# Maxima by one-input reductions, statistics in other steps and second-norm factors in one place, in an attention and mixture-of-experts kernel

## The chip, the cores and the metric

The kernel runs on one core of a Trainium2 chip. The metric is the device time of one execution in microseconds (us); the time of a kernel is the median of several runs. Besides these runs there is one profiled execution, from which every view of the trace is taken; its own time stands beside its span below. The engines are called TensorE (PE, its weight loads PEld), VectorE (DVE), ScalarE (ACT), GpSimd (POOL) and SyncE (SP, which issues most transfers).

## The reference

```python
x = layernorm(x + attention(x))          # x: 4 x 1024 x 256, 16 heads of 16
x = layernorm(x + experts(x))            # 8 experts, top 2, capacity 640
# attention: softplus magnitudes times cos/sin of positions make q and k of 32 elements a head
scores = einsum('bhsd,bhtd->bhst', q_embed, k_embed) / D ** 0.5
out = einsum('bhst,bhtd->bhsd', softmax(scores), v)
# experts: a token goes to its two best experts, if these have a free slot
h = gelu(einsum('ecd,edh->ech', buf, w1) + b1)
out = einsum('ech,ehd->ecd', h, w2) + b2
```

Everything is float32. The layernorm has no learned scale. The second layernorm of a token that no expert took is again a norm of an already normed row, so that it needs only one factor for a row.

## The kernel before, in words

**Attention.** The work is cut into 32 units: 4 batches of 8, each with two heads and all 1024 queries in two halves. A unit has eight steps, one for each block of 128 keys; the loop over `NS` writes the order of every engine by hand. A step of unit u does, in this order: two halves of the scores of the *next* unit, with queries on the partitions (`score_half`, L701), a tile of this unit's scores with keys on the partitions (`key_scores`, L728), a third score half, the second tile, a fourth score half; then `exponentials` adds minus the maximum of each query to the tiles by a matmul with two rows (L743) and takes the exponential on ScalarE (L750); then `weighted_values` (L764, 16 matmuls) of the step before.

The scores of the next unit serve only to find each query's maximum: VectorE reduces each half from PSUM (L705, 512 keys to one number, negated) into the small tile `nm`. The score halves, and every other small matmul (embeddings, values, projections, transposes), share three PSUM banks that go round (`bank`), so that a score half waits until VectorE has reduced the one of three banks before.

In step 6 of a unit `max_parts` takes the smaller of the two halves' negated maxima (L711), rounds it to the float32r format of the matmul (L712), and takes the rest that the rounding left (L713); all three are on VectorE, 16 elements a partition. In step 7 `max_rows` transposes both parts (L719), and ScalarE copies them out of PSUM (L721) for the next unit's L743. `max_parts(0)` and `max_rows(0)` also stand ahead of the first step.

**Work beside it.** The table `todo` gives pieces of other work to fixed steps (unit p of the batch, step c). `embedding` makes the next batch's q and k in three stages: matmuls (L367) with ScalarE's softplus, then GpSimd's products and rounded parts (L390 to L405, operations of 128x512 on SBUF), then stores. `values` makes v (L336). `over_sums` divides by the softmax sums. `project` (L455) adds the output projection of two row tiles to the rows `x1` on VectorE (L463); `statistics` takes mean and variance of two row tiles (two of L472 and two of L473). For the second half of the heads of batch b-1 the four projections stand at (0,7), (1,0), (1,1), (1,2) of batch b, and the four `statistics` at (1,0), (1,1), (1,3), (1,4). Projections of the first half of the heads stand at (6,0) to (6,3), in the last batch at (5,2) to (5,5).

The list `FINISH` runs `finish_batch(b-1)` piece by piece after the `todo` of a step, from (1,5) on: the first norm's root (L495 to L502), the normed rows (L511), their transposes and the router's matmul, the softmax over experts, the two best experts, the slots by prefix sums (L600 to L606), and the scatters of rows into the experts' slots. At (3,7) it also starts `second_factors` (L665 to L669), which makes the factor of the second norm, `again`, for the rows that no expert takes; at (5,4) come the rest of it (L671 to L674) and the first scatter. Each of (5,4) to (6,3) converts the slot numbers of one row tile into integers on VectorE (L644) and issues two scatters from GpSimd (L646).

**End of attention.** For the last batch all this runs with no attention beside it: projections, statistics, and two interleaved `finish_batch` over four row tiles each (with `rotate`, which makes it use five banks, and convert the slot numbers at once); `second_factors` comes last in each.

**Experts.** For each of 8 experts the slots are loaded (L1071), transposed, multiplied by w1, gelu, w2. `without_experts` multiplies the normed rows by `again` (L1157) and stores them; rows of experts replace theirs later by scatters (L1191).

Of the kernel before, what the change touches and what calls it, by code (L numbers as in the profile page):

```python
# [10 lines left out]
F32 = mybir.dt.float32  # L11
F32R = mybir.dt.float32r
I32 = mybir.dt.int32
U32 = mybir.dt.uint32
AF = mybir.ActivationFunctionType
ALU = mybir.AluOpType
AX = mybir.AxisListType
# [3 lines left out]
P = 128  # L21
# [7 lines left out]
def kernel(  # L29
# [18 lines left out]
    nc = tc.nc  # L48
    B, S, DIM = x.shape
    E, _, HID = w1.shape  # L50
    HD = 16
    NT = S // P
# [49 lines left out]
    with ExitStack() as actx:  # L102
# [203 lines left out]
            return ps_3.tile([P, 512], F32, tag="bank", name=name)  # L306


        xts, qks, oss, ots, stats = {}, {}, {}, {}, {}
        nums, sums, routed, xt1s = {}, {}, {}, {}  # L310

        def transpose_x(b, i, rotate=False, copy=nc.scalar.copy):
# [152 lines left out]
            )  # L465

        def statistics(b, j):
            if b not in stats:
                stats[b] = small.tile([P, NT, 2], F32, tag="mv", name=f"mv_{b}")
            for t in (2 * j, 2 * j + 1):  # L470
                bs = small.tile([P, 6], F32, tag="bs", name=f"bs_{b}_{t}")
                nc.vector.bn_stats(bs, x1[:, b * NT + t, :])  # L472
                nc.vector.bn_aggr(stats[b][:, t, :], bs)  # L473

        def finish_batch(b, rotate=False, lo=0, n=NT):


            mv = stats[b][:, lo : lo + n, :]

            def some(name, shape):  # L480
                if (b, name) not in routed:
# [5 lines left out]
            def t1(name):  # L487
                return some(name, (NT,))[:, lo : lo + n]
# [2 lines left out]
                return some(name, (NT, E))[:, lo : lo + n, :]  # L491


            r, v, t = t1("ln_r"), t1("ln_v"), t1("ln_t")
            nc.vector.tensor_scalar(v, mv[:, :, 1], EPS, None, ALU.add)  # L495
            nc.scalar.activation(r, v, AF.Ln)
            nc.scalar.activation(r, r, AF.Exp, scale=-0.5)
# [131 lines left out]
            nc.vector.tensor_reduce(  # L629
                held[:, tiles, DIM : DIM + 2].rearrange("p t k -> p k t"), both, AX.X, ALU.add  # L630
            )
            second = second_factors(b, lo, n, r, v, t)
            if not rotate:
                next(second)
            yield
            if not rotate:
                next(second, None)
            for st in range(n):
                if st:
                    yield  # L640
                t = b * NT + lo + st
                if not rotate:

                    nc.vector.tensor_copy(scatter_idx[:, :, t], to[:, :, st])  # L644
                for k in range(2):
                    nc.gpsimd.indirect_dma_start(  # L646
                        out=scatter_views[2 * t + k],
                        out_offset=bass.IndirectOffsetOnAxis(
                            ap=scatter_idx[:, k, t : t + 1], axis=0
                        ),  # L650
                        in_=held[:, t, :],
                        in_offset=None,
                        bounds_check=SLOTS - 1,
                        oob_is_err=False,
                    )
            if rotate:
                yield
                for _ in second:
                    pass

        def second_factors(b, lo, n, r, v, t):


            more = again[:, b * NT + lo : b * NT + lo + n]
            nc.vector.tensor_tensor(v, r, r, ALU.mult)  # L665
            nc.vector.tensor_tensor(v, v, stats[b][:, lo : lo + n, 1], ALU.mult)
            nc.vector.tensor_scalar(v, v, EPS, None, ALU.add)
            nc.scalar.activation(more, v, AF.Ln)
            nc.scalar.activation(more, more, AF.Exp, scale=-0.5)  # L669
            yield  # L670
            nc.vector.tensor_tensor(t, more, more, ALU.mult)  # L671
            nc.vector.tensor_tensor(t, t, v, ALU.mult)
            nc.vector.tensor_scalar(t, t, -0.5, 1.5, ALU.mult, ALU.add)
            nc.vector.tensor_tensor(more, more, t, ALU.mult)  # L674

        zero = aconst.tile([P, ROW], F32, name="zero")
        nc.gpsimd.memset(zero, 0.0)
# [14 lines left out]
        def score_half(u, k, j):  # L692


            i, s = divmod(k, 4)
            if u not in nms:
                nms[u] = small.tile([P, 2, 4, 4], F32, tag="nm", name=f"nm_{u}")
            qk, h = qks[u], s % 2
            lo = HS * (s // 2) + P * i
            ps = bank(f"s_{u}_{k}_{j}")  # L700
            nc.tensor.matmul(  # L701
                ps, qk[:, 2 * h, lo : lo + P], qk[:, 2 * h + 1, j * HS : (j + 1) * HS],
                start=True, stop=True,
            )
            nc.vector.tensor_reduce(nms[u][:, j, i, s : s + 1], ps, AX.X, ALU.max, negate=True)  # L705

        def max_parts(u):

            nm = nms.pop(u)
            m = m_sb[u % 2].rearrange("p i (s c) -> p i s c", c=32)  # L710
            nc.vector.tensor_tensor(nm[:, 0], nm[:, 0], nm[:, 1], ALU.min)  # L711
            nc.vector.tensor_copy(m.bitcast(F32R)[:, :, :, 0], nm[:, 0])  # L712
            nc.vector.tensor_tensor(m[:, :, :, 1], nm[:, 0], m[:, :, :, 0], ALU.subtract)  # L713

        def max_rows(u, rotate=False):

# [135 lines left out]
        def run(pieces):  # L852
            next(pieces, None)
# [10 lines left out]
        for b in range(1, B):  # L864
            pieces = over_sums(b - 1, 1)
            for c in (1, 2, 5, 6):
                at(b, 0, c, run, pieces)
            for j, (p, c) in enumerate(((0, 7), (1, 0), (1, 1), (1, 2))):
                at(b, p, c, project, b - 1, 1, j)
            for j, (p, c) in enumerate(((1, 0), (1, 1), (1, 3), (1, 4))):  # L870
                at(b, p, c, statistics, b - 1, j)
        FINISH = [(1, 5), (1, 6), (1, 7), (2, 0), (2, 1), (2, 2), (2, 3), (2, 4), (2, 5), (2, 7)]
        FINISH += [(3, c) for c in range(NT)]
# [34 lines left out]
        with tc.manual_schedule():  # L908
            bias_angles()
            once("k", 0)  # L910
            for i in range(2):
                transpose_x(0, i, rotate=True)
            nc.scalar.dma_start(wv_sb, wv)
            for w in "kq":
                load_twice(w, 1, nc.scalar)
            key_table(0)
            once("q", 0)

            def first(w, h):
                tab = cs if w == "q" else kt0  # L920
                return embedding(0, 0, w, h, fast=True, tab=tab, pauses=(KC - 1,))

            k0, q0, k1, q1 = first("k", 0), first("q", 0), first("k", 1), first("q", 1)
            run(k0)
            for i in range(2, 4):
                transpose_x(0, i, rotate=True, copy=nc.vector.tensor_copy)
            for work in (q0, k0, q0, k0, k0):
                run(work)
            load_qk(0, halves[0], "k")
            for work in (k1, q0, q0):  # L930
                run(work)
            load_qk(0, halves[0], "q", nc.gpsimd)
            key_table(1)
            for work in (k1, q1, q1, k1, k1):
                run(work)
            load_qk(0, halves[1], "k")
            for work in (q1, q1):
                run(work)
            load_qk(0, halves[1], "q", nc.gpsimd)
            once("k", 1)  # L940
            once("q", 1)
            for h in range(2):
                values(0, 0, h, rotate=True)
            load_qk(1)
            for h in range(2):
                store_table(0, h, cs[:, :, halves[h]])
                store_table(1, h, kt0[:, :, halves[h]])
            late_constants()
            works = [embedding(0, 1, "q", h, tab=cs, pauses=(0, 1)) for h in range(2)]
            vals = [values_in_two(0, 1, h) for h in range(2)]  # L950
            beside = {n: (run, works[0]) for n in (3, 5, 6, 11, 17)}
            beside |= {n: (run, vals[i]) for n, i in ((8, 0), (10, 0), (14, 1), (16, 1))}
            beside |= {n: (second_key_table, h) for n, h in ((1, 0), (12, 1))}
            beside |= {n: (run, works[1]) for n in (20, 22, 23)}
            at(0, 0, 1, run, works[1])
            at(0, 0, 2, run, works[1])
            n = 0
            for queries in range(2):
                for keys in range(2):
                    for i in range(8):  # L960
                        score_half(0, 4 * (i // 2) + 2 * queries + i % 2, keys)
                        if n in beside:
                            f, *args = beside[n]
                            f(*args)
                        n += 1
            max_parts(0)
            max_rows(0, rotate=True)


        NS = B * NU * NT  # L970
        finishing = {}
        with tc.manual_schedule():
            for n in range(NS):
                u, c = divmod(n, NT)
# [13 lines left out]
                if ahead:  # L988
                    score_half(v, k, 0)
                    score_half(v, k, 1)  # L990
                tiles = [key_scores(u, c, 0)]
                if ahead and not third_last:
                    score_half(v, k + 1, 0)
# [10 lines left out]
                if n > 0:  # L1004
                    weighted_values(*divmod(n - 1, NT))
                if c == 6 and u + 1 < B * NU:
                    max_parts(u + 1)
                if c == 7 and u + 1 < B * NU:
                    max_rows(u + 1)
                if c == 1 and u > 0 and not by_rows(u - 1):  # L1010
# [10 lines left out]
        with tc.manual_schedule():  # L1021
# [27 lines left out]
                run(one)  # L1049
            for _ in two:  # L1050
                pass
            run(one)
            nc.scalar.preload_act_table_set("gelu_and_others")


# [292 lines left out]
```

## Time and profile before

| what | us |
|---|---|
| median of 3 runs (lowest to highest) | 1449.51 (1448.92 to 1450.37) |
| the profiled execution | 1455.47 |
| its span, first to last instruction | 1453.6 |
| of the span: start, up to the first step's L743 | 60.9 |
| the 256 steps, to the end of the last L764 | 60.9 to 1103.5 |
| from there to the first transpose of slots (L1082) | 1103.5 to 1153.9 |
| experts | 1153.9 to 1453.6 |
| granted TensorE clock, mean of the span | 0.972 |

A row of groups reads: line, engine, operation, output<-input, output shape<-input shape, count | busy us, mean ns of one | idle time of the engine just before, and what ended most of it. A row of the timeline reads: start in us, length in us, engine, line, operation, names and shapes, count, and in brackets the idle time before it with its releaser. Rows of neighbouring instructions of one kind are merged there. A busy TensorE is not TensorE at its peak, since the ends of matmuls are modelled. `min/median/max` of a line are the lengths of its single instructions.

The length of a step can be read from the timeline as the time from one first L743 to the next. The shortest with scores of a next unit is 3.50 us, in about 100 steps; at c = 7, which has `max_rows`, it is 3.87.

### The profile page before, as it was taken

How to read it: one execution, taken by the hardware profiler on the slowest of the kernel's cores; microseconds unless marked ns; L12 is line 12 of the kernel's file. 1: busy time of each engine (PE TensorE's matmuls, PEld its weight loads, DVE VectorE, ACT ScalarE, POOL GpSimd, SP SyncE). 2: the span in 40 equal slices, each digit the busy share in tenths (PEclk: the TensorE clock that was granted, in tenths of full speed). 3: DMA queues.
4: the chain of work that ended last, by engine and by line, in shares of the span. 5: the costliest groups of instructions: out<-in, count | busy, mean ns of one | idle time of the engine just before them, and what ended most of it. 6: DMA issues, size and time to landing. Idle time of an engine off the chain costs nothing. (4 is left out here: it accounts for less than half of the span.)

```text
span 1453.6 us, 24361 instructions
## 1 busy us (share of the span) xinstructions
PE 1367.7 (94%) x9314; PEld 859.4 (59%) x9314; DVE 921.3 (63%) x1990; ACT 727.5 (50%) x944; POOL 411.2 (28%) x436
## 2 busy tenths in 40 slices
PE   5899999999999999999999999999996399999996
PEld 3455555655665565555555555555543277777775
DVE  7767766667877766787767677887644433333334
ACT  5365666565566556546674654655553122222221
POOL 5640043340002637000064530000210414444542
PEclk8899999999999999999999999999998599999998
DMA  7956367373444646454465352224210436433211
GB/s 240 261 177 173 100 188 205 87 228 107 126 120 113 213 133 180 121 151 102 129 185 181 105 176 74 63 63 118 90 64 0 139 112 212 115 120 131 73 44 43
DMA packets 107315, 191.23 MB, mean 132 GB/s; under 512 B 19633, under 2 KB 56178, under 8 KB 107072
## 3 DMA queue, kind: packets, MB, share of 16 engines
q1 hardware_dynamic: 96192, 167.80, 39.7%
q0 software_dynamic: 9888, 20.01, 4.5%
q10 hardware_dynamic: 1120, 1.87, 0.4%
q8 instruction: 73, 1.20, 0.4%
q14 instruction: 42, 0.34, 0.1%
HBM read 119.32 MB, written 73.63 MB: 133 GB/s over the span
## 5 line engine op out<-in xcount | busy, mean ns | idle before, releaser
L705 DVE TENSOR_REDUCE nm<-s 128x1 f32<-128x512 f32 x1024 | 644.8, 684 | 230.4 <-PE s L701 212.6
L750 ACT ACTIVATE pt<-st 128x1024 f32<-128x1024 f32 x512 | 496.3, 1021 | 393.7 <-PE st L743 378.9
L701 PE MATMUL s<-qk 128*128 128x512 f32 x1024 | 391.5, 441 | 25.6 <-DVE nm L705 14.5
L728 PE MATMUL st<-qk 128*128 128x512 f32 x1024 | 308.4, 401 | 3.5 <-ACT pt L750 3.4
L764 PE MATMUL av<-pt,va 128*32 128x256 f32 x4096 | 275.5, 386 | 0.5 <-ACT pt L750 0.5
L701 PEld LDWEIGHTS s<-qk 128*128 128x128 f32 x1024 | 180.2, 191 | 138.3 <-DVE nm L705 62.4
L728 PEld LDWEIGHTS st<-qk 128*128 128x128 f32 x1024 | 183.3, 189 | 67.1 <-ACT pt L750 32.7
L764 PEld LDWEIGHTS av<-pt,va 128*32 128x32 f32 x4096 | 107.1, 109 | 107.8 <-issue 62.4
L646 POOL DMA_INDIRECT slots_in<-held,scatter_idx x64 | 62.7, 980 | 304.4 <-DVE scatter_idx L644 226.4
L390 POOL TENSOR_TENSOR soft_q<-y_q,soft_q 128x512 f32<-128x512 f32 x14 | 17.9, 1282 | 447.3 <-ACT soft_q L386 447.2
L1249 PE MATMUL op<-w,h 128*128 128x256 f32 x640 | 144.1, 379 | 0.0
L1230 PE MATMUL hp<-slots_t,w 128*128 128x320 f32 x512 | 139.9, 434 | 0.0
L743 PE MATMUL st<-mt,ones_r 2*128 2x512 f32 x1024 | 129.6, 495 | 0.7 <-ACT mt L721 0.7
L1249 PEld LDWEIGHTS op<-w,h 128*128 128x128 f32 x640 | 119.4, 190 | 15.9
L1230 PEld LDWEIGHTS hp<-slots_t,w 128*128 128x128 f32 x512 | 97.7, 191 | 40.0 <-ACT slots_t L1083 0.3
L743 PEld LDWEIGHTS st<-mt,ones_r 2*128 2x128 f32 x1024 | 49.0, 181 | 89.5 <-issue 88.1
L1237 ACT ACTIVATE h<-hp,b_sb 128x640 f32<-128x640 f32 x64 | 50.8, 794 | 86.6 <-PE hp L1230 73.3
L1264 DVE TENSOR_TENSOR o<-op,b_sb 128x256 f32<-128x256 f32 x35 | 14.9, 425 | 93.3 <-PE op L1249 88.9
L1265 ACT ACTIVATE o<-o,w 128x256 f32<-128x256 f32 x35 | 17.8, 507 | 103.1 <-issue 71.9
L1267 POOL DMA_INDIRECT y_rank<-o,rows x35 | 35.9, 1025 | 98.4 <-ACT slots_t L1083 42.2
L1191 POOL DMA_INDIRECT out_dram<-row,rows x40 | 41.0, 1025 | 44.6 <-DVE row L1146 14.3
L396 POOL TENSOR_TENSOR e_k<-soft_k,tab_k 128x512 f32<-128x512 f32 x28 | 35.4, 1286 | 46.3 <-DMA tab_k<-table 45.8
(210 smaller groups left out, 1030.6 us busy)
## 6 DMA issues: line engine op xcount, KB each, us to landing
qk<-embed_q SPq DMA_DIRECT2D x248, 128.0 KB
qk<-embed_k SPq DMA_DIRECT2D x124, 256.0 KB
embed_k<-parts_k SPq DMA_DIRECT2D x64, 256.0 KB
w<-in_w_dram SPq DMA_DIRECT2D x16, 1024.0 KB
embed_q<-parts_q SPq DMA_DIRECT2D x56, 256.0 KB
y_rank<-zero SPq DMA_DIRECT2D x8, 1024.0 KB
tab_k<-table SPq DMA_DIRECT2D x14, 512.0 KB
tab_q<-table SPq DMA_DIRECT2D x12, 512.0 KB
```

The lines of the kernel that those rows point to most:

```text
L646: nc.gpsimd.indirect_dma_start(out=scatter_views[2 * t + k], out_offset=bass.IndirectOffsetOnAxis(ap=scatter_idx[:, k, t : t + 1], axis=0) ...
L701: nc.tensor.matmul(ps, qk[:, 2 * h, lo : lo + P], qk[:, 2 * h + 1, j * HS : (j + 1) * HS], start=True, stop=True,)
L705: nc.vector.tensor_reduce(nms[u][:, j, i, s : s + 1], ps, AX.X, ALU.max, negate=True)
L728: nc.tensor.matmul(ps[:, f, :], qk[:, 2 * h + 1, c * P : (c + 1) * P], qk[:, 2 * h, f * HS : (f + 1) * HS], start=True, stop=False,)
L743: nc.tensor.matmul(tiles[h][:, f, :], ones_r[rows, :], mts[u][rows, :], start=False, stop=True,)
L750: nc.scalar.activation(pt, tiles[h], AF.Exp)
L764: nc.tensor.matmul(av[32 * s : 32 * (s + 1), cols], va[f][:, c, 2 * p + h, :], pt[h][:, s // 2, cols], start=(c == 0 and n == 0), stop=(c ...
L1191: nc.gpsimd.indirect_dma_start(out=out_views[t], out_offset=bass.IndirectOffsetOnAxis(ap=to[:, 0, t : t + 1], axis=0), in_=row[:, t, :], i ...
L1230: nc.tensor.matmul(ps[:, i, 0:half], w1_sb[:, k, c * P : (c + 1) * P], s_t[:, k, i * half : (i + 1) * half], start=(k == 0), stop=(k == KC ...
L1237: nc.scalar.activation(h_t[:, c, :].rearrange("p (i n) -> p i n", i=2), ps[:, :, 0:half], AF.Gelu, bias=b1_sb[:, e, c : c + 1],)
L1249: nc.tensor.matmul(ps, h_t[:, c, t * P : (t + 1) * P], w2_sb[:, c, :], start=(c == 0), stop=(c == HC - 1),)
L1267: nc.gpsimd.indirect_dma_start(out=y_views[e * ST + t], out_offset=bass.IndirectOffsetOnAxis(ap=to[:, 1, t : t + 1], axis=0), in_=o_sb, in ...
```

## The change

- `max_parts`: the two halves of `nm` now lie side by side, and one reduction of 128x32 to 128x16 takes the smaller. ScalarE makes the rounded part and a rounded negated copy beside the unrounded one, and in the next step, after the first two score halves, VectorE adds the pairs by a second reduction, which gives the rest.
- The conversion of slot numbers at (5,4) to (6,3) becomes a reduction over one element.
- `statistics` stand at (1,2), (1,3), (1,4), (1,5).
- The variances of all 32 row tiles and the roots of the first norm are kept in two tiles for all batches, and `second_factors` runs once for all 32 row tiles, at the end of attention.

```diff
+        stats = aconst.tile([P, B * NT, 2], F32, name="stats")
+        roots = aconst.tile([P, B * NT], F32, name="roots")
...
-            r, v, t = t1("ln_r"), t1("ln_v"), t1("ln_t")
+            r, v, t = roots[:, b * NT + lo : b * NT + lo + n], t1("ln_v"), t1("ln_t")
...
-            second = second_factors(b, lo, n, r, v, t)
-            if not rotate:
-                next(second)
-            yield
-            if not rotate:
-                next(second, None)
+            yield
...
-                    nc.vector.tensor_copy(scatter_idx[:, :, t], to[:, :, st])
+                    nc.vector.tensor_reduce(
+                        scatter_idx[:, :, t], to[:, :, st : st + 1], AX.X, ALU.max
+                    )
...
-            if rotate:
-                yield
-                for _ in second:
-                    pass
-
-        def second_factors(b, lo, n, r, v, t):
-
-
-            more = again[:, b * NT + lo : b * NT + lo + n]
-            nc.vector.tensor_tensor(v, r, r, ALU.mult)
-            nc.vector.tensor_tensor(v, v, stats[b][:, lo : lo + n, 1], ALU.mult)
+
+        def second_factors():
+
+            v, t = (small.tile([P, B * NT], F32, name=f"second_{i}", bufs=1) for i in range(2))
+            nc.vector.tensor_tensor(v, roots, roots, ALU.mult)
+            nc.vector.tensor_tensor(v, v, stats[:, :, 1], ALU.mult)
             nc.vector.tensor_scalar(v, v, EPS, None, ALU.add)
-            nc.scalar.activation(more, v, AF.Ln)
-            nc.scalar.activation(more, more, AF.Exp, scale=-0.5)
-            yield
-            nc.vector.tensor_tensor(t, more, more, ALU.mult)
+            nc.scalar.activation(again, v, AF.Ln)
+            nc.scalar.activation(again, again, AF.Exp, scale=-0.5)
+            nc.vector.tensor_tensor(t, again, again, ALU.mult)
             nc.vector.tensor_tensor(t, t, v, ALU.mult)
             nc.vector.tensor_scalar(t, t, -0.5, 1.5, ALU.mult, ALU.add)
-            nc.vector.tensor_tensor(more, more, t, ALU.mult)
+            nc.vector.tensor_tensor(again, again, t, ALU.mult)
...
-            nc.vector.tensor_tensor(nm[:, 0], nm[:, 0], nm[:, 1], ALU.min)
-            nc.vector.tensor_copy(m.bitcast(F32R)[:, :, :, 0], nm[:, 0])
-            nc.vector.tensor_tensor(m[:, :, :, 1], nm[:, 0], m[:, :, :, 0], ALU.subtract)
+            both = small.tile([P, 4, 4, 2], F32, tag="nm_parts", name=f"nm_parts_{u}")
+            nc.vector.tensor_reduce(both[:, :, :, 0], nm, AX.X, ALU.min)
+            nc.scalar.copy(m.bitcast(F32R)[:, :, :, 0], both[:, :, :, 0])
+            nc.scalar.activation(
+                both.bitcast(F32R)[:, :, :, 1], both[:, :, :, 0], AF.Copy, scale=-1.0
+            )
+            yield
+            nc.vector.tensor_reduce(m[:, :, :, 1], both, AX.X, ALU.add)
...
-            for j, (p, c) in enumerate(((1, 0), (1, 1), (1, 3), (1, 4))):
+            for j, (p, c) in enumerate(((1, 2), (1, 3), (1, 4), (1, 5))):
                 at(b, p, c, statistics, b - 1, j)
...
                     score_half(v, k, 0)
                     score_half(v, k, 1)
+                if parts:
+                    run(parts)
+                    parts = None
                 tiles = [key_scores(u, c, 0)]
...
                 if c == 6 and u + 1 < B * NU:
-                    max_parts(u + 1)
+                    parts = max_parts(u + 1)
+                    run(parts)
...
             for _ in two:
                 pass
-            run(one)
+            second_factors()
```

More of the change, by code (lines that the diff above doesn't have):

```diff
@@ L306, in bank @@
             return ps_3.tile([P, 512], F32, tag="bank", name=name)
-        xts, qks, oss, ots, stats = {}, {}, {}, {}, {}
+        xts, qks, oss, ots = {}, {}, {}, {}
+        stats = aconst.tile([P, B * NT, 2], F32, name="stats")
+        roots = aconst.tile([P, B * NT], F32, name="roots")
         nums, sums, routed, xt1s = {}, {}, {}, {}
@@ L467, in statistics @@
         def statistics(b, j):
[L468 to L473, printed above, removed]
+            for t in (b * NT + 2 * j, b * NT + 2 * j + 1):
+                bs = small.tile([P, 6], F32, tag="bs", name=f"bs_{t}")
+                nc.vector.bn_stats(bs, x1[:, t, :])
+                nc.vector.bn_aggr(stats[:, t, :], bs)
         def finish_batch(b, rotate=False, lo=0, n=NT):
-            mv = stats[b][:, lo : lo + n, :]
+            mv = stats[:, b * NT + lo : b * NT + lo + n, :]
             def some(name, shape):
@@ L696, in score_half @@
             if u not in nms:
-                nms[u] = small.tile([P, 2, 4, 4], F32, tag="nm", name=f"nm_{u}")
+                nms[u] = small.tile([P, 4, 4, 2], F32, tag="nm", name=f"nm_{u}")
             qk, h = qks[u], s % 2
@@ L704, in score_half @@
             )
-            nc.vector.tensor_reduce(nms[u][:, j, i, s : s + 1], ps, AX.X, ALU.max, negate=True)
+            nc.vector.tensor_reduce(nms[u][:, i, s, j : j + 1], ps, AX.X, ALU.max, negate=True)
         def max_parts(u):
@@ L965 @@
                         n += 1
-            max_parts(0)
+            for _ in max_parts(0):
+                pass
             max_rows(0, rotate=True)
         NS = B * NU * NT
-        finishing = {}
+        finishing, parts = {}, None
         with tc.manual_schedule():
```

## The prediction

> I write a step of the attention stage as (p, c): unit p of a batch, key block c; batch b is named where it matters. A step's length is the time between the first L743 matmuls of two neighbouring steps in the timeline.
>
> **What bounds the kernel now.** First the page's busy times and costliest groups:
>
> ```profile
> PE 1367.7 (94%) x9314; PEld 859.4 (59%) x9314; DVE 921.3 (63%) x1990; ACT 727.5 (50%) x944; POOL 411.2 (28%) x436
> ...
> L705 DVE TENSOR_REDUCE nm<-s 128x1 f32<-128x512 f32 x1024 | 644.8, 684 | 230.4 <-PE s L701 212.6
> L701 PE MATMUL s<-qk 128*128 128x512 f32 x1024 | 391.5, 441 | 25.6 <-DVE nm L705 14.5
> ```
>
> TensorE is the bound; among its waits, the one that this change can touch is L701's for L705: a score bank that VectorE has not yet reduced. The chain of waits covers only the last 25 us (output rows), so I went to the groups of all lines, looking at means that are far above what the same work takes elsewhere:
>
> ```profile
> L712 DVE CAST m<-nm 128x16 fp32r<-128x16 f32 x32 | 12.4, 388 | 1.1
> L713 DVE TENSOR_TENSOR m<-nm,m 128x16 f32<-128x16 f32 x32 | 10.8, 338 | 1.1
> L807 DVE RECIPROCAL den<-den 128x64 f32<-128x64 f32 x7 | 3.8, 544 | 0.8 <-DMA den<-sums 0.8
> L711 DVE TENSOR_TENSOR nm<-nm 128x16 f32<-128x16 f32 x32 | 9.6, 301 | 1.1
> L674 DVE TENSOR_TENSOR again<-again,ln_t 128x8 f32<-128x8 f32 (+1 forms) x5 | 2.9, 577 | 0.2
> L502 DVE TENSOR_TENSOR ln_r<-ln_r,ln_t 128x8 f32<-128x8 f32 (+1 forms) x5 | 0.8, 166 | 0.2
> ```
>
> L674 and L502 do the same arithmetic, yet one averages 577 ns and the other 166. By line, L711 takes 174/176/940 ns (min/median/max), L712 181/184/1233, L713 187/192/1202, L644 156/159/1299. The timeline shows where the long ones lie, here unit 7 of batch 2:
>
> ```profile
> 849.14 0.60 DVE L711 TENSOR_TENSOR nm<-nm 128x16 f32<-128x16 f32 x1
> ...
> 849.69 2.51 POOL L405 TENSOR_TENSOR parts_k<-e_k,parts_k 128x512 fp32r<-128x512 f32 x2
> 849.78 1.23 DVE L712 CAST m<-nm 128x16 fp32r<-128x16 f32 x1
> ...
> 851.05 1.20 DVE L713 TENSOR_TENSOR m<-nm,m 128x16 f32<-128x16 f32 x1
> 852.16 1.87 DVE L705 TENSOR_REDUCE nm<-s 128x1 f32<-128x512 f32 x3
> ...
> 852.90 0.49 PE L701 MATMUL s<-qk 128*128 128x512 f32 x1 [1.40 <-DVE nm L705]
> ```
>
> Each small VectorE operation lasts until a GpSimd operation beside it ends; the four reductions queue behind, and TensorE stands 1.40 us. The other kind of hole:
>
> ```profile
> 355.13 0.69 DVE L463 TENSOR_TENSOR held<-po,held 128x512 f32<-128x512 f32 x1 [1.41 <-PE po L455]
> ...
> 355.74 0.42 DVE L472 BATCH_NORM_STATS2 bs<-held 128x6 f32<-128x256 f32 x1
> ...
> 356.72 0.18 DVE L473 BATCH_NORM_AGGREGATE mv<-bs 128x2 f32<-128x6 f32 x1
> 356.82 1.85 DVE L705 TENSOR_REDUCE nm<-s 128x1 f32<-128x512 f32 x3
> ...
> 357.54 0.49 PE L701 MATMUL s<-qk 128*128 128x512 f32 x1 [0.82 <-DVE nm L705]
> ```
>
> No GpSimd is involved: the projection's addition comes late (it waits for TensorE), and the statistics behind it delay the next reductions.
>
> **What a step tolerates.** A plain step is 3.50 us; its four reductions take 2.48. Counted from L743, the fourth of the old step ends at +0.96, the first of the new one starts at +1.98: 1.02 us of VectorE are free. The fourth score needs the first one's bank: in the row above L701 starts 0.72 after the reductions (356.82 to 357.54), against +3.18 in a plain step, so they may be 0.48 late. Extra VectorE work up to 1.5 us costs nothing. That is why most long L711 to L713 are hidden: at (4,6) and (6,6), which carry an embedding's matmuls, steps of 5.20 are as long as at (4,2) and (6,4), without one.
>
> **The change part by part**
>
> *Statistics, from (1,0), (1,1), (1,3), (1,4) to (1,2) to (1,5).* Each issues four VectorE instructions (355.74 to 356.90, some 1.1 us) and no DMA. (1,0) and (1,1) of batches 1 to 3 last 5.43; a projection without statistics, at (6,1), takes 4.44. Six times 0.99 is 5.9 us. At (1,2), 6.13 long, the value matmuls (1.95 us) run behind the projection: the addition ends at 366.69, the next reduction starts at 368.02, and 1.1 fit between. At (1,3) and (1,4) such work stands today in steps of 3.50. (1,5) gets it beside L495 (0.2): 1.3 of the 1.5. ScalarE's L496 waits for L495, at about +2.3; its exponentials end at +2.55 anyway. Cost 0; without that cover 0.3 each. SP's queue has loads and zero fills at (1,4) and (1,5), which wait for none of this; GpSimd's has nothing there.
>
> *Second factors.* Today nine instructions per batch. Those at (3,7), two ScalarE ones among them, cost nothing (3.87, like any (p,7)). L671 to L674 and L644 at (5,4) do: 5.71 in batch 1 and 6.10 in batch 2, against 3.49 in batch 0, where they are absent; (5,5) follows with 3.87 and 5.07 against 3.50. Batch 3: 5.14 against 4.44 at its neighbour with the same projection. Gain (2.22 + 0.37) + (2.61 + 1.57) + 0.70 = 7.5 us. They come back once, 32 wide, after the last routing: 7 x 0.19 (row of 128x32) and 2 x 0.23 on ScalarE, some 2 us from 1137.7. The consumers, L1157, stand until the scatters have read their rows (1142.80 to 1149.39), and the expert stage waits for slots landing at 1153.9. GpSimd's last scatters wait for L629, which comes before; at (5,4) GpSimd's first scatter waits for L644, which now comes earlier. So 0; if not covered, +2.
>
> *Maxima.* Three VectorE operations per unit become one-input reductions, two of them, and two ScalarE operations. No tiny reduction of SBUF runs beside a GpSimd tensor operation here. Nearest row: L807, one input, SBUF to SBUF, 542/542/553 ns, though three of its seven lie beside L390 in the timeline. [...] Bounds: 0.17 to 0.2 us as L580 and L1096, or as long as L711's mean 0.30; I take 0.19. Gain at (7,6): 4.40, 5.05 and 5.16 become 3.50, that is 0.90 + 1.55 + 1.66 = 4.1. Batch 2's (7,7), 5.43, becomes 3.87: 1.6 more. At the start, max_parts(0) holds L719 from 57.33 to 59.13, 1.80 us; new chain 0.19 + 0.2 + 0.2 + 0.19 and three hand-overs of 0.05 is 0.93 (ScalarE idles there): 0.9.
>
> *The price of ScalarE.* Its small operations take 0.20 (L496) to 0.27 (L537). Both casts queue behind the exponentials, +2.55, and end at about +3.0. Behind them wait embedding reads of PSUM, which start 1.0 after ScalarE falls idle at (6,6), and the next exponentials at +4.1: 0. VectorE's second reduction comes in (p,7) after two score reductions, +3.2: 0.2 spare. Were it late, the third and fourth reductions are held; (p,7) is 3.87 long, and TensorE wants the third one's bank only 1.4 after its normal end.
>
> *scatter_idx.* Same count, 0.16 to 0.2 instead of a stall; counted at (5,4).
>
> [...] The long (7,7) of batch 2 and 1.2 us of (5,5) in batch 2 are not VectorE waits: the granted clock is 0.68 and 0.67 over these steps. [...] The gaps ahead of them are 1.40 and 2.35 us. [...] By the row, the falls directly follow two of the longest gaps, and the windows view has a clock of 1.00 in 100 to 700 and 900 to 1075 us, 0.98 only in between. I take the row.
>
> **Sum.** 5.9 + 7.5 + 4.1 + 1.6 + 0.9 = 20.0, less nothing: the span 1453.6 becomes 1433.6, and the profiled execution 1455.5 becomes 1435.5. The median of the runs shown, 1449.5, lies 6.0 below that execution; the steps are the same, so I take the difference over: 1429.5. What is late next in the freed steps is TensorE itself, at 3.50.
>
> **Rivals**
>
> 1. *Part of it stays* (0.16): the clock falls anyway, or the new reductions are stretched too. Then 2.8 is lost, or the 0.9 of the start and 1.1 of L644 at (5,4): about 1432.
> 2. *Another wait takes over at (5,4) and (7,6)* (0.06). For it: DMA is 0.64 to 0.74 busy in these holes. Against: L701 names L705, and its operands are loaded two units ahead. Only the statistics pay: 1443.6.
> 3. *ScalarE's casts come late* (0.03), slower. Place: VectorE, in order, stands at the second reduction of (p,7). It decides beyond 0.2 + 1.4 = 1.6 us of lateness; break-even at 20.0/31 = 0.65 more per unit. With the casts behind two further exponentials, 3 us late: 31 x 1.4 = 43, less 20: 1473. Against: the casts stand ahead of those exponentials in ScalarE's order.
> 4. *It cancels* (0.03): the same lateness of about 2.2 us: 1449.5.
>
> **How the numbers follow.** The forecast has 0.72. About 0.2% (3 us) is what a measurement of this kernel tells from no change. Faster is 0.72 + 0.16 + 0.06 = 0.94, same 0.03, slower 0.03. The range: down to 1425.5, since the clock's windows (3.4 us at half rate) can fall 1.7 us better on either side of the routing pause; up to 1437.5, past rival 1 with stalls of 3 us left and a second lost window.
>
> **What would show it.** (1,0), (1,1) at 4.44; (5,4), (5,5), (7,6) at 3.50 in batches 1 and 2; (1,3) to (1,6) still at 3.50; small reductions with a maximum near 0.2; no clock below 1 between 70 and 1090 us. Wrong if (p,7) exceeds 3.87, if VectorE waits for ScalarE there, or if the pause after attention grows.

## The result and the profile after

| what | us |
|---|---|
| kernel before, median of 5 runs beside it (lowest to highest) | 1450.37 (1448.92 to 1453.40) |
| kernel after, median of 5 runs | 1434.52 (1433.47 to 1435.21) |
| ratio, 95% interval | 0.9878 [0.9863, 0.9892] |
| profiled execution of after; its span | 1435.0; 1433.2 |
| predicted time (range); predicted span | 1429.5 (1425.5 to 1437.5); 1433.6 |

The kernel became 1.2% faster: 17.7 us by the ratio, while the two medians lie 15.9 apart. The predicted span was met to 0.4 us; the predicted median lies 5 us too low. The busy times and groups of the page after, the lines that answer to those of before (L697 was L705, L693 was L701):

```profile
PE 1360.3 (95%) x9314; PEld 856.8 (60%) x9314; DVE 888.3 (62%) x1930; ACT 732.8 (51%) x1000; POOL 410.5 (29%) x436
...
L697 DVE TENSOR_REDUCE nm<-s 128x1 f32<-128x512 f32 x1024 | 646.3, 684 | 240.5 <-PE s L693 232.2
...
L693 PE MATMUL s<-qk 128*128 128x512 f32 x1024 | 387.9, 438 | 13.6 <-DVE parts_q L408 8.3
```

What TensorE waits ahead of a score half falls from 25.6 to 13.6 us, and VectorE's reduction no longer leads that list (14.5 before; 2.1 by the groups of all lines). VectorE itself is 33 us less busy. The steps and the pause after them, by the windows view (borders, length; busy us and instructions of PE, PEld, DVE, ACT, POOL; granted clock; DMA share; GB/s), before:

```profile
60.90:1103.50 1042.60, 1024.49 (x7844) 596.61 (x7844) 735.71 (x1362) 608.80 (x732) 240.46 (x231) 0.99 0.47 135
1103.50:1153.90 50.40, 16.18 (x90) 11.39 (x90) 28.68 (x129) 7.88 (x20) 15.61 (x16) 0.64 0.15 49
```

and after:

```profile
60.10:1082.70 1022.60, 1017.45 (x7844) 594.37 (x7844) 704.33 (x1310) 614.09 (x788) 241.67 (x232) 1.00 0.48 138
1082.70:1133.10 50.40, 16.13 (x93) 11.08 (x91) 28.49 (x123) 7.56 (x18) 15.56 (x16) 0.61 0.15 49
```

The gain is in the 256 steps (20.0 us) and ahead of them (0.8); the experts take 299.7 us before and 300.1 after. The pause, where the second factors now stand, is as long as it was: they are hidden there. The small operations, by the single line's view (ns, min/median/max):

```profile
L704 DVE TENSOR_REDUCE nm_parts<-nm x32: 186/186/189, 58.0 to 1050.6; 128x16 f32<-128x32 f32 x32
```

```profile
L710 DVE TENSOR_REDUCE m<-nm_parts x32: 176/178/189, 58.6 to 1052.5; 128x16 f32<-128x32 f32 x32
...
  ACT nm_parts L706: 2.0, 2
```

No maximum above 0.19 us where L711 to L713 reached 0.94 to 1.23, although 17 of these 64 instructions ran beside a GpSimd tensor operation. VectorE waited for ScalarE's pair of casts only twice: 0.39 us at the start and 1.62 in the last unit, where it has no scores to reduce. The statistics' place, (1,0) of batch 1, which the prediction showed at 355 us, is now:

```profile
353.60 0.69 DVE L466 TENSOR_TENSOR held<-po,held 128x512 f32<-128x512 f32 x1 [1.43 <-PE po L458]
354.21 2.48 DVE L697 TENSOR_REDUCE nm<-s 128x1 f32<-128x512 f32 x4
```

The reductions follow the projection's addition at once, and the step fell from 5.43 to 4.38. Step (5,4) of batch 1, where the rest of the second factors stood, before:

```profile
502.25 1.18 DVE L674 TENSOR_TENSOR again<-again,ln_t 128x8 f32<-128x8 f32 x1
...
504.16 0.50 PE L701 MATMUL s<-qk 128*128 128x512 f32 x1 [1.95 <-DVE nm L705]
```

and after:

```profile
495.98 0.15 DVE L640 TENSOR_REDUCE scatter_idx<-to 128x2 uint32<-128x2 f32 x1
497.06 1.89 DVE L697 TENSOR_REDUCE nm<-s 128x1 f32<-128x512 f32 x3 [0.94 <-PE s L693]
```

TensorE waited for VectorE there; now VectorE waits for TensorE, and the step fell from 5.71 to 3.51. Unit 7 of batch 2, the place that the prediction showed at 849 us, now, VectorE, then GpSimd, then TensorE of the timeline:

```profile
835.40 0.19 DVE L704 TENSOR_REDUCE nm_parts<-nm 128x16 f32<-128x32 f32 x1
836.36 1.29 DVE L697 TENSOR_REDUCE nm<-s 128x1 f32<-128x512 f32 x2 [0.78 <-PE s L693]
```

```profile
835.11 1.16 POOL L406 CAST parts_k<-e_k 128x512 fp32r<-128x512 f32 x2
```

```profile
837.58 0.40 PE L693 MATMUL s<-qk 128*128 128x512 f32 x1
```

The reduction ends at 835.59, in the middle of GpSimd's casts (835.11 to 836.27), VectorE again waits for TensorE (0.78), and the fourth score starts with no wait in brackets. The step fell from 5.16 to 3.51. Not all is free of waits. One that was not there before, in (0,2) of batch 2:

```profile
853.46 0.55 DVE L804 RECIPROCAL den<-den 128x64 f32<-128x64 f32 x1 [1.97 <-DMA den<-sums]
...
854.61 0.49 PE L693 MATMUL s<-qk 128*128 128x512 f32 x1 [0.76 <-DVE nm L697]
```

VectorE waits 1.97 us at the division by the softmax sums until these are loaded, and its next three score reductions begin only behind it, at 853.93. The step took 0.55 more here and 1.0 more in batch 3.

### The profile page after: what moved, and what is told of

Read it like the earlier page. It is cut to its first block, busy times and chain, and to the rows that moved or that the text cites. A ratio compares the mean times of both kernels' runs of the same rounds, so it can differ in the third digit from the quotient of the medians.

```text
span 1433.2 us, 24396 instructions
## 1 busy us (share of the span) xinstructions
PE 1360.3 (95%) x9314; PEld 856.8 (60%) x9314; DVE 888.3 (62%) x1930; ACT 732.8 (51%) x1000; POOL 410.5 (29%) x436
## 5 line engine op out<-in xcount | busy, mean ns | idle before, releaser
L697 DVE TENSOR_REDUCE nm<-s 128x1 f32<-128x512 f32 x1024 | 646.3, 684 | 240.5 <-PE s L693 232.2
L693 PE MATMUL s<-qk 128*128 128x512 f32 x1024 | 387.9, 438 | 13.6 <-DVE parts_q L408 8.3
L693 PEld LDWEIGHTS s<-qk 128*128 128x128 f32 x1024 | 179.6, 190 | 121.4 <-DVE nm L697 49.9
L1251 PEld LDWEIGHTS op<-w,h 128*128 128x128 f32 x640 | 119.4, 190 | 15.9
```

The costliest lines, as they stand in the source:

```text
L693: nc.tensor.matmul(ps, qk[:, 2 * h, lo : lo + P], qk[:, 2 * h + 1, j * HS : (j + 1) * HS], start=True, stop=True,)
L697: nc.vector.tensor_reduce(nms[u][:, i, s, j : j + 1], ps, AX.X, ALU.max, negate=True)
L1251: nc.tensor.matmul(ps, h_t[:, c, t * P : (t + 1) * P], w2_sb[:, c, :], start=(c == 0), stop=(c == HC - 1),)
```

## The experiments

Theory 1 is the prediction's: each part takes away its own stalls, which are a constant of the kernel. Its rival, theory 2: the stalls change from one execution to the next, so that neither their sizes nor the 6.0 us between one execution and a median can be carried over. After the first four runs came theory 3: converting the slot numbers by a copy, beside GpSimd's scatters, holds the chip up, and only a kernel without it keeps its gains. The first four runs below were made on one chip, the next four on a second, the last four on a third; the kernel before had a median of 1455.47 us (37 runs, 1452.08 to 1461.82) on the first, 1453.06 (23 runs) on the second, 1454.35 (25 runs) on the third. A "hole" is a place where VectorE begins its reductions more than 0.3 us after the scores are done, with nothing in front of them.

**The kernel before, once more.**

> The kernel before, unchanged, profiled once more. The question: its first profiled execution took 1455.5 us, 5.1 over its median of 1450.4, so that a sum made against it promised 20 us where the runs gave 15.9. Theory 1: that one execution carried stalls that a usual one has not (half clock behind the two longest gaps in batch 2, 2.8 us; waits at (5,7) and (6,3) of batch 3, 1.9 us). Then this profiled execution takes 1449 to 1452, without some of those four, and all the other long steps, (1,0), (1,1), (5,4), (7,6), have the lengths they had within 0.1 us. Theory 2 (rival): the stalls beside GpSimd differ from one execution to the next as a whole; then (5,4) and (7,6) differ by 0.5 us and more. Ratio to before 1.000 within 0.001.

1454.29 us, ratio 0.9989 [0.9974, 1.0004]. The profiled execution took 1458.3, not the 1449 to 1452 that theory 1 expected. Its steps sum to 1041.7 (1042.6), but the stalls sit elsewhere: (5,4) of batch 2 takes 5.67 where it took 6.10, (7,6) of batch 2 4.04 for 5.16, (7,7) of batch 1 5.43 for 3.87, and the half clock falls at 509, 591 and 779 us in place of 773 and 855. Theory 2 holds for each stall; that their sum came out alike is one pair of executions. What made this one longer is the start: up to the first step's L743 it took 64.8 us, in place of 60.9.

**Statistics alone.**

```diff
-            for j, (p, c) in enumerate(((1, 0), (1, 1), (1, 3), (1, 4))):
+            for j, (p, c) in enumerate(((1, 2), (1, 3), (1, 4), (1, 5))):
```

> The kernel before with only the four statistics moved to (1,2) to (1,5). Both theories: (1,0) and (1,1) of batches 1 to 3 fall from 5.43 to 4.38, six times 1.05: 6.3 us less, in the runs too, since no GpSimd work is beside these steps. If the gain of the steps is given back later (a wait on a transfer), it is less than 5.

1450.3 us, ratio 0.9961 [0.9946, 0.9976], 5.7 us less. (1,0) and (1,1) of batches 1 to 3 take 4.37 to 4.38; (1,6) is 0.17 longer in each. This term of the sum (5.9) stands.

**Second factors alone.**

```diff
-            second = second_factors(b, lo, n, r, v, t)
...
+            second_factors()
```

> The kernel before with only the factors of the second norm made once for all tiles; the slot numbers are still converted by a copy. Theory 1: (5,4) of batches 1 and 2 fall to 3.5 to 4 us, 4 to 5 us less, and 0.7 in batch 3: 4.5 to 6 us in the runs. Theory 2: 2 to 4 us. The pause after attention is unchanged (50.5 us) by both; a rival in which the factors made there cost something gives 2 us more for it.

1455.13 us, ratio 0.9998 [0.9986, 1.0011]: no gain, a miss. And yet (5,4) of batches 1 and 2 is at 3.50 as expected. The profile shows where it went, in step (5,6) of batch 1:

```profile
510.20 0.71 PE L691 MATMUL s<-qk 128*128 128x512 f32 x2
...
511.36 0.97 POOL L642 DMA_INDIRECT slots_in<-held,scatter_idx  x1 [0.30 <-issue]
513.40 0.58 ACT L348 COPY va<-vp 128x512 f32<-128x512 f32 x1 [3.90 <-remote]
513.44 1.89 DVE L695 TENSOR_REDUCE nm<-s 128x1 f32<-128x512 f32 x3 [3.66 <-remote]
...
514.04 0.74 PE L691 MATMUL s<-qk 128*128 128x512 f32 x2 [2.20 <-ACT va L348]
```

The scores are done at 510.9; ScalarE and VectorE both start at 513.4, late and together, while GpSimd issues scatters, and the profile names no engine as releaser ("remote"). This step and (5,6) of batch 2 lost 2.5 us each; in batch 3 (5,7) and (6,0), at 5.60 and 5.06, lost 0.6 and 1.6 more. This led to theory 3.

**Maxima alone.**

```diff
-            nc.vector.tensor_tensor(nm[:, 0], nm[:, 0], nm[:, 1], ALU.min)
...
+            nc.vector.tensor_reduce(both[:, :, :, 0], nm, AX.X, ALU.min)
...
+            nc.vector.tensor_reduce(m[:, :, :, 1], both, AX.X, ALU.add)
```

> The kernel before with only max_parts changed to two one-input reductions and ScalarE's casts. Theory 1: (7,6) of batches 0 to 2 falls to 3.5, 4.1 us, and the start gains 0.3 to 0.8: 4 to 5 us in the runs. Theory 2: 2 to 3 us. If ScalarE's casts cost steps of their own, less than 2.

1451.46 us, ratio 0.9968 [0.9955, 0.9982], 4.7 us less. (7,6) takes 3.50, 3.79 and 3.50, (7,7) of batch 2 3.86; a new hole at (5,6) of batch 3 (4.55 in place of 3.49) and longer (5,5) in batches 1 and 2 (5.00 and 6.03, at half clock) take some of it back in the profiled execution.

**Conversion alone.**

```diff
-                    nc.vector.tensor_copy(scatter_idx[:, :, t], to[:, :, st])
+                    nc.vector.tensor_reduce(
+                        scatter_idx[:, :, t], to[:, :, st : st + 1], AX.X, ALU.max
+                    )
```

> The kernel before with only the conversion of the slot numbers changed, from a copy to a one-input reduction over one element. The factors alone gained nothing in the runs and the profile of that kernel has new holes of 2.5 us at (5,6), where TensorE's scores are done and VectorE and ScalarE start on them only 3 us later, while GpSimd issues scatters; such holes lie at (5,5) to (6,3) in every profile of a kernel with the copy and in none of the changed kernel. Theory 3 (new): the copy beside scatters in issue holds the chip up for 1 to 3 us at changing places; then this one edit takes 2 to 6 us off the runs and narrows their spread of 7 to 12 us to under 4, although its own time in the profile is worth 1.1. Theory 1: the edit is worth about 1 us.

1451.75 us, ratio 0.9991 [0.9979, 1.0003], 1.3 us, and its runs spread over 7.9 us: what theory 3 expected of it alone is missed. Its profile has no hole, and (5,4) falls to 4.73 and 5.03.

**The kernel after with the copy back.**

```diff
-                    nc.vector.tensor_reduce(
-                        scatter_idx[:, :, t], to[:, :, st : st + 1], AX.X, ALU.max
-                    )
+                    nc.vector.tensor_copy(scatter_idx[:, :, t], to[:, :, st])
```

> The changed kernel with the copy to integers put back in place of the reduction over one element, all else as changed. Theory 3: 3 to 8 us slower than the changed kernel on the same chip, with holes again at (5,5) to (6,3) and a spread of over 5 us. Theory 1: at most 1.2 us slower.

1434.89 us, ratio 0.9882 [0.9843, 0.9920]. The kernel after on this chip, two runs further down, has 0.9876: the intervals overlap. The copy takes up to 0.68 us, and no hole follows. On this chip the copy by itself does not hold the kernel up.

**The division one step later.**

```diff
-            for c in (1, 2, 5, 6):
+            for c in (1, 3, 5, 6):
```

> The changed kernel with the reciprocal of the softmax sums of the second heads at (0,3) in place of (0,2). Its profile shows VectorE waiting there for a load that now lands 1.5 to 2.0 us after VectorE reaches it, and steps of 4.05 and 4.51 in batches 2 and 3. If that is where part of the gain was given back, (0,2) is 3.50 again and the kernel is 1.0 to 1.6 us faster than the changed one. If the wait moves on to (0,3) or to the next load, 0 to 0.5.

1434.59 us, ratio 0.9879 [0.9843, 0.9916], no gain. (0,2) is at 3.49 in batches 2 and 3, but (0,5) of batch 1 takes 4.46 in place of 3.49: the wait moved to the load of the reciprocals, `r`, ahead of the multiplication (VectorE waits 1.72 us there).

**The kernel after, once more.**

> The changed kernel, unchanged, on the same chip as the three others, for comparison with them. Ratio to before 0.985 to 0.990; spread of its runs under 3 us; steps as in its first profile within 0.1 us, except that the waits for a load at (0,2) may differ.

1433.37 us, ratio 0.9876 [0.9840, 0.9913]; span 1430.9. Here (0,2) takes 4.02 in batch 1 and 3.48 in the others. So this wait, too, changes its place between executions, and e7 could not settle it.

**Factors and conversion together.**

```diff
-            second = second_factors(b, lo, n, r, v, t)
...
-                    nc.vector.tensor_copy(scatter_idx[:, :, t], to[:, :, st])
+                    nc.vector.tensor_reduce(
+                        scatter_idx[:, :, t], to[:, :, st : st + 1], AX.X, ALU.max
+                    )
...
+            second_factors()
```

> The kernel before with two parts of the change: second factors made once, and the slot numbers converted by a reduction; maxima and statistics as before. Theory 'the copy hides it' (the factors' gain was there in e3 but holes beside the scatters took it back, and these need the VectorE copy): (5,4), (5,5) of batches 1 and 2 at 3.50, no step between (5,5) and (6,3) over 4.0, and the runs about 6 us below the kernel before (6.0 from the steps of e3 plus some 0.3 to 1). Theory 'they are nearly nothing in runs': the sum of e3 and e5, 0.3 + 1.3 = 1.6 us below. Between 3 and 5 us would leave it open.

1445.62 us, ratio 0.9940 [0.9921, 0.9959]: 8.7 us less, where the two alone, on the first and the second chip, add up to 1.6. Its profile, at the place of the hole in the run of the factors alone:

```profile
509.29 0.97 POOL L644 DMA_INDIRECT slots_in<-held,scatter_idx  x1 [0.31 <-issue]
...
510.00 2.08 DVE L697 TENSOR_REDUCE nm<-s 128x1 f32<-128x512 f32 x3 [1.12 <-PE s L693]
```

The same steps and the same scatters, and VectorE is released by the score it waits for. (5,4) and (5,5) are at 3.50, and there is no hole. This is what a theory expects in which the copy brings the holes. But the run of the factors alone was made on another chip, so that the chip is a rival that this pair can't exclude.

**The second reduction as an operation of two inputs.**

```diff
-            nc.scalar.activation(
-                both.bitcast(F32R)[:, :, :, 1], both[:, :, :, 0], AF.Copy, scale=-1.0
-            )
...
-            nc.vector.tensor_reduce(m[:, :, :, 1], both, AX.X, ALU.add)
+            nc.vector.tensor_tensor(
+                m[:, :, :, 1], both[:, :, :, 0], m[:, :, :, 0], ALU.subtract
+            )
```

> The kernel after, with the second reduction of the maxima (step 7) replaced by a VectorE subtraction of two inputs, 128x16; ScalarE's negated copy is left out. Theory of the one-input form: this operation, and no other, is stretched beside GpSimd's 128x512 tensor operations, to a maximum of 0.9 to 1.3 us in the units with an embedding beside (7,7), while L704's reduction stays below 0.19. In time it costs nothing that the runs can tell (within 0.3% of the kernel after's ratio): the reductions behind it in a step (p,7) may be 1.4 us late. Rival, 'the form doesn't matter': its maximum stays below 0.25. Rival, 'no slack at (p,7)': the steps with a stretched subtraction exceed 3.87 by what it is longer, up to 1 us each, some 3 to 6 us in all.

```profile
L707 DVE TENSOR_TENSOR m<-nm_parts,m x32: 178/182/1237, 59.6 to 1051.7; 128x16 f32<-128x16 f32 x32
```

```profile
L704 DVE TENSOR_REDUCE nm_parts<-nm x32: 185/186/188, 59.2 to 1050.0; 128x16 f32<-128x32 f32 x32
```

The subtraction ran beside a GpSimd tensor operation in seven places and took 0.35 to 1.24 us in five of them (the longest at (4,7) of batch 0, not at (7,7) as expected). The reductions of the kernel after, beside the same GpSimd lines, take 0.189 us at most. It is not the number of inputs alone: L712 of the kernel before, a cast with one input, reached 1.23. The time is 1436.09 us, ratio 0.9873 [0.9843, 0.9903], as that of the kernel after; the step of the 1.24 takes 4.01, 0.14 more than 3.87. In a step of 3.87, behind two score reductions, even this is nearly covered.

**Extra VectorE work, two and three reductions of 128x512 in step 6.**

```diff
+                    for _ in range(2):
+                        idle = small.tile([P, 1], F32, tag="idle", name=f"idle_{u}_{_}")
+                        nc.vector.tensor_reduce(idle, wv_sb, AX.XY, ALU.max)
```

> The kernel after with extra work whose result nothing uses: two VectorE reductions of a 128x512 SBUF tile in step 6 of each unit, ahead of the maxima, about 0.62 each, 1.24 us. The prediction's tolerance: extra VectorE work up to 1.5 us in a step costs nothing; with the maxima's reduction (0.19) this is 1.43. Expected: (p,6) of the plain units at 3.50 to 3.55, the runs within 1.5 us of the kernel after. Rival, 'the tolerance is smaller' (1.0, the free time of VectorE alone): 0.4 in each of some 20 plain units, 8 us slower.

> The same with three such reductions, 1.86 us, with the maxima's 0.19 some 2.05: over the tolerance of 1.5 by 0.55. Expected: plain (p,6) at 4.0 to 4.1, TensorE waiting for L697's reduction there, and with some 20 such units the runs about 11 us above the kernel after (8 to 17, if the longer steps of the other units pay too). Rival, 'TensorE's place in the order hides more' (tolerance of 2.1 or more): within 1.5 us of the kernel after. Rival, tolerance 1.0: 1.05 a unit, 20 to 30 us.

The diff is that with two; with three the range is 3. Both add work that nothing uses. With two: 1441.94 us, ratio 0.9911 [0.9878, 0.9944]. The preceding run, as fast as the kernel after, was made on the same chip; against it this is 5.9 us more, where up to 1.5 was expected: missed. The plain units are as expected, (2,6) of batches 1 to 3 at 3.53 to 3.54, (7,6) at 3.48 to 3.51. Eleven others pay, 5.8 us in all, for instance (1,6) of batch 1 with 4.33. VectorE there:

```profile
378.29 1.27 DVE L1010 TENSOR_REDUCE idle<-wv_sb 128x1 f32<-128x512 f32 x2
...
379.57 0.16 DVE L500 TENSOR_TENSOR ln_t<-roots 128x8 f32<-128x8 f32 x1
...
380.25 1.28 DVE L697 TENSOR_REDUCE nm<-s 128x1 f32<-128x512 f32 x2
```

The first norm's root (L500 to L503, 0.7 us) stands in the same step. From 378.29 to 380.25 VectorE is held 1.96 us, over the tolerance of 1.5; the step is 0.84 longer, which leaves 1.1 for the tolerance here. The expectation counted the maxima and forgot what else stands in step 6: the root at (1,6), a multiplication by the reciprocal sums at (0,6) and, in batch 3, at (4,6), pieces of `finish_batch` at (3,6) and, in batch 3, at (5,6). With three, 1451.70 us, ratio 0.9985 [0.9975, 0.9995], 15.6 us more than that run (8 to 17 expected). (2,6) of batch 1, a plain one, takes 4.13, and TensorE shows the wait:

```profile
413.35 1.86 DVE L1010 TENSOR_REDUCE idle<-wv_sb 128x1 f32<-128x512 f32 x3
415.13 0.17 DVE L704 TENSOR_REDUCE nm_parts<-nm 128x16 f32<-128x32 f32 x1
```

```profile
415.96 0.50 PE L693 MATMUL s<-qk 128*128 128x512 f32 x1 [0.36 <-DVE nm L697]
```

The four operations hold VectorE from 413.35 to 415.30, 1.95 us, and plain steps are 0.40 to 0.63 longer, so the tolerance is 1.3 to 1.55 there: the prediction's 1.5 is near the upper end. Rivals at 1.0 and 2.1 both fall for plain steps.

## Why the prediction was right, and where it was not

| step of the prediction | predicted | profile after | that part alone, in runs |
|---|---|---|---|
| statistics | 5.9 | 6.3 | 5.7 [3.5, 7.9] |
| second factors and conversion | 7.5 | 7.5 | 8.7 [6.0, 11.5] |
| maxima at (7,6) and (7,7) | 5.7 | 5.6 | 4.7 [2.6, 6.5], with the start |
| start | 0.9 | 0.75 | |
| everything else | 0 | 0.3 | |
| sum | 20.0 | 20.4 | 19.1, together 17.7 [15.7, 19.9] |

Microseconds saved; the last column is one minus the ratio, times the median of before on that chip. The sum of 20.0 answers to two single executions, which differ by 20.4; against the 17.7 of the runs it lies just above the interval.

That the start came out as forecast is luck. Its operations of `max_parts(0)`, up to the first transpose, fell from 1.85 us (57.33 to 59.18) to 0.82 (57.99 to 58.81), but they began 0.66 later, and the start of one and the same kernel before took 60.9 and 64.8 in two executions.

**Which stalls go.** (5,4) and (5,5) of batches 1 and 2 are at 3.49 to 3.51 and (7,6) at 3.50 to 3.51; (5,4) of batch 3 is at 4.44, (7,7) of batch 2 at 3.87, (1,0) and (1,1) at 4.38. (1,3) to (1,6) stayed at 3.50. Each part alone shows its own, and the parts add up if factors and conversion are taken as one.

**The form of the operation.** The value taken for the reductions was 0.19, the measured ones 0.186 and 0.178; ScalarE's casts took 0.22 and 0.23, within the 0.20 to 0.27 assumed. The run with two inputs shows that a subtraction is stretched, up to 1.24 us, where a reduction in its place takes 0.189 at most. Why the one form is stretched and the other is not, no run shows.

**The clock.** The prediction put the two falls of the clock down to the gaps of 1.40 and 2.35 us ahead of them, and counted the 2.8 us that they cost as gained: 1.6 at (7,7) and 1.2 at (5,5) of batch 2. The windows view of before, over the two stretches at half clock:

```profile
772.50:776.20 3.70, 3.70 (x25) 2.21 (x22) 2.27 (x5) 1.94 (x2) 2.93 (x3) 0.54 0.16 55
854.50:858.10 3.60, 3.60 (x18) 2.79 (x11) 1.43 (x3) 1.96 (x3) 0.00 (x0) 0.53 0.78 215
```

and of after, over all steps but the first:

```profile
70.00:1082.00 1012.00, 1006.89 (x7818) 588.94 (x7817) 696.99 (x1299) 612.15 (x786) 239.56 (x230) 1.00 0.48 136
```

With these two gaps gone, the falls are gone. Had the clock fallen all the same, the 2.8 us would have been lost. The other traces agree: all ten falls between 75 us and the end of the steps, in six profiles, come behind gaps of 0.98 to 2.39 us, and in the eight profiles without a fall no gap exceeds 1.14. What the runs can't say is which gap lets the clock fall: in before gaps of 1.30 and 1.95 us let it stand, in the run of the factors alone one of 2.20.

**What is late next.** "TensorE itself" holds in the freed steps, but not everywhere. The loads of the softmax sums now come late at (0,2), in one or two batches of an execution (1.6 us given back), and the first two steps are 0.5 longer. On the other side batch 3's (5,7) and (6,3), holes that the prediction did not name, fell by 1.1 and 0.8. These nearly cancel, and that the sum came out within 0.4 us is partly this luck.

**The step that failed** is the last one: "The median of the runs shown, 1449.5, lies 6.0 below that execution; the steps are the same, so I take the difference over". That execution is not one of the runs shown (1448.9 to 1450.4). The profiled execution of after lies 0.5 above its median, not 6.0, and this one term makes the 5 us by which the median was missed. Medians of the kernel before lie between 1449.5 and 1455.5 from one group of runs to the next, single runs between 1448 and 1462; the nine runs of the kernel after lie between 1432.6 and 1435.2. So the gain was 15.0 over the median shown, 15.9 over the one beside it, and 19.7 on the second chip (17.7 and 18.0 by the ratios of the last two).

What the 6.0 consisted of is not shown. Part of it can be stalls that the change takes away, since the stalls, the clock falls and the holes of the kernel before differ from one execution to the next. But the two profiled executions of before differ by 3.9 us in the start, which the change barely touches, and by 0.9 in the steps; and the run with three extra reductions, whose steps show no hole and no fall of the clock, still takes 1449.3 to 1454.8 over 20 runs. That the median fell inside the range is luck too: its upper end was argued from stalls that stay and a lost clock window, and it was not these that moved the median.

**Where the gain of the factors alone went** is not settled. Holes stand in the five profiles of kernels that have the copy and other parts of before (twice the kernel before, statistics, factors and maxima alone), and in none of the eight that convert by a reduction; factors alone gain nothing on the first chip, with the conversion 8.7 on the third. But the kernel after with the copy back has none either, and another division fits all fourteen profiles as well. In the five with holes 41 to 53 of TensorE's 2399 semaphore records (by which a trace shows who releases whom) are missing, in the nine others one at most; 15 to 18 of those missing lie after attention (counted against the conversion alone), where before and that kernel do the same work, which speaks against the copy as what loses them. Four of the five come from the first chip, the fifth is the profile of before, whose chip is not on record; and no kernel with the copy and other parts of before was profiled on the second or third chip. So the chip, or the recording of the trace itself, explains the holes as well as the copy does, and what holds VectorE and ScalarE there stays open. The run that would decide is the factors alone, again, on the third chip. A kernel with its scatters moved to another place, or issued by another queue, was not tried; neither was the kernel after with ScalarE's casts given back to VectorE.

## What to carry to other kernels

A tiny operation costs what it holds up (here three VectorE operations of 0.60 to 1.23 us in place of 0.18 to 0.19, and TensorE 1.40 us behind them): look for small groups whose mean is far above what the same work takes elsewhere, and find the engine beside which they last. Work out how late the next critical operation may be, and count everything that the step already holds before calling an addition free. Compare profile with profile and median with median: the difference between one execution and the runs of another group is not a constant of the kernel, and a change need not leave it as it was. Before two runs on different chips are set against each other, repeat one of them on the other's chip.

## What the runs showed of the hardware

- A 128x16 VectorE operation beside GpSimd's 128x512 operations: 0.18 us as a reduction (maximum 0.189 in 64, 17 of them beside such an operation), up to 1.24 with two SBUF inputs, up to 1.23 as a cast.
- TensorE's clock was halved for some 3.4 us after idle gaps of 1.40 and 2.35 us, and stayed at 1.00 for 1012 us in which no gap exceeded 0.76; gaps of 1.95 and 2.20 us did not always bring a fall.
- Beside GpSimd's scatters, VectorE began its reductions 0.7 to 2.9 us after the scores were done by the trace, in five of fourteen profiles; in those five semaphore records are missing too. The cause is open.
